# Expert tiles beyond 36 put behind a branch, and none begun in the first unit of a pass

## Chip, core and metric

The kernel runs on one core of a Trainium2 chip. The metric is the device time of one execution in microseconds. The profile is of one execution, taken by the hardware profiler. The engines are TensorE (PE; its weight loads are PEld), VectorE (DVE), ScalarE (ACT), GpSimd (POOL) and SyncE (SP), which issues most of the DMA transfers.

## What is computed

The reference runs two transformer layers over 8 x 256 tokens of width 512, in fp32. Layer 0 adds a linear attention with decays (32 heads of 128, gated, normalized over all heads) and a mixture of experts to its input. Layer 1 adds a small attention and a mixture of 64 low-rank maps.

```
x = x + _L0_attn_ref(xn, ...) + _L0_ffn_ref(xn, ...)
xn = _layernorm(x, axis=-1)
x = x + _L1_attn_ref(xn, ...) + _L1_ffn_ref(xn, ...)
```

The change touches the mixture of experts of layer 0. Each of the 2048 tokens picks 2 of 16 experts:

```
logits = xt @ router_w + router_b
scores = jax.nn.softmax(logits.astype(jnp.float32), axis=-1) + router_bias
g = scores.reshape(T, GROUPS, E // GROUPS)
_, gidx = jax.lax.top_k(g.max(axis=-1), LIM)
...
_, idx = jax.lax.top_k(masked, K)
...
h = jax.nn.silu(xt @ w1 + b1) * (xt @ w2 + b2)
return (y + ge[:, None] * (h @ w3 + b3), None)
```

The reference lets every expert see every token and weights the results with a gate that is zero for all but two experts. The kernel computes only the chosen pairs. How many tokens an expert gets depends on the data.

## The kernel before

**Opening.** The kernel normalizes the tokens, scores them, picks two experts each, and computes the two shared experts. Then it sorts the 4096 (token, expert) pairs into slots, expert after expert, each expert's share rounded up to tiles of 128 slots (lines 495 to 579). Whatever the counts are, no more than NMT = (2048 x 2 + 16 x 127) // 128 = 47 tiles are needed. `ends` (line 546) holds, for each expert, the number of tiles up to and including its own; the last of them is the number of tiles in use. `rows_` and `own_` name the expert whose weights and bias a tile takes; a tile past the last one in use takes expert 15.

**Main loop.** The attention of layer 0 runs in NCH = 4 passes of 512 tokens (i), each with NG = 8 units of four heads (g), and each unit with seven outer products in the order p1, p2, p6, p5, p3, p7, p4 (k = 0 to 6, line 1318). An outer product multiplies one combination of weight blocks with seven combinations of token blocks, on PE at line 735. The weights of two outer products ahead are requested on SP (lines 709 to 712, a ring of three buffers `w`). ACT and DVE empty PSUM, POOL and DVE add the results up. A unit's scores, attention and output projection (lines 857 to 870, 948, 968) are cut into pieces which `later(after, f)` puts on a list; `slot()` (line 755), called once for each small product, takes due pieces from that list, one at a time or two where the list is long. Pieces with names in the tuple at line 762 do not count toward that number.

The instructions of ACT and POOL keep the order in which the code issues them; those of the other engines are ordered by the compiler from the same sequence, by their dependences.

**Expert tiles.** They are such pieces too. `expert(j)` (line 1187) makes an `Expert`, whose two gathers on POOL bring 128 token rows (`xe`) and the weights of the expert (`we`) to a buffer of the pool `stage`, of which there are two; ten slots later `turn` transposes the tokens on PE (line 786), `bias` gathers the bias rows on POOL (792), `up` multiplies (804), with Silu on ACT and one operation on DVE, and `down` multiplies again (816), adds the bias on DVE and stores the result to the rows of tile j of `yd` in DRAM (822). Later, `gather` reads the rows of `yd` that a token's slots name. The same two `stage` buffers also serve the block sums of pass 0, `spare8()` (line 657: at a pass's end, in `load_sum`), and `low_sums`.

The lines 1327 to 1330 hand the tiles out: from the first unit of pass 1 on, at each unit's first outer product, two of them, or three in units 1 to 7 of pass 1; in a first unit (g = 0) they begin 24 slots later than elsewhere. This gives 23 tiles in pass 1, 16 in pass 2 and 8 in units 0 to 3 of pass 3.

**Around a pass's end.** The last unit of a pass queues `combine` (POOL, on the accumulator `acc`), `finish` (DVE, line 646, reads acc) and `store`, which run in the next pass's first unit. There is one `acc`; the next pass first writes it with an ACT copy at line 956.

Of the kernel before, what the change touches and what calls it, by code (L numbers as in the profile page):

```python
# [12 lines left out]
I32 = mybir.dt.int32  # L13
# [7 lines left out]
P = 128  # L21
CH = 512
NCH = NT // CH
# [4 lines left out]
NG = H // HG  # L28
# [4 lines left out]
E, GROUPS, INTER = 16, 4, 128  # L33
# [4 lines left out]

NMT = (NT * TOP + E * (P - 1)) // P
NSLOT = NMT * P  # L40
READ = 32
WROW = 2 * NC * INTER + C + 2
K, TOPK, RANK, SCALING = 64, 16, 16, 2.0
# [27 lines left out]
def block_kernel(  # L71
# [24 lines left out]
    nc = tc.nc  # L96
# [5 lines left out]
    const = ctx.enter_context(tc.tile_pool(name="const", bufs=1))  # L102
# [43 lines left out]
    def once(shape, name, dtype=FP):  # L146
        return work.tile(shape, dtype, tag=name, name=name, bufs=1)
# [31 lines left out]
    dram = ctx.enter_context(tc.tile_pool(name="dram", bufs=1, space=bass.MemoryType.DRAM))  # L179
    yd = dram.tile([NSLOT, C], FP, name="yd")  # L180
    gd = [dram.tile([K, 1, CH], FP, name=f"gd{i}") for i in range(NCH)]
# [10 lines left out]
    xr = [dram.tile([P, TPC, C], FP, name=f"xr{i}") for i in range(NCH)]  # L192
    table = dram.tile([NSLOT, SAME], I32, name="table")
    none = once([P, NMT * SAME], "none", I32)
# [11 lines left out]
    for n in range(WARM):  # L206
# [12 lines left out]
        out=before, in_=before, pattern=[[1, E], [-1, E]], compare_op=ALU.is_gt,  # L219
# [11 lines left out]
        out=dist[:, 0:S], in_=dist[:, 0:S], pattern=[[1, S]], compare_op=ALU.is_ge,  # L231
# [238 lines left out]
    for i in range(NCH):  # L470
        nc.sync.dma_start(
            out=xnd[i * CH : (i + 1) * CH, :].rearrange("(t p) c -> p t c", p=P), in_=xns[i]
# [25 lines left out]
    own_ = const.tile([P, NMT], I32, name="own_")  # L498
    whose = [const.tile([P, n], I32, name=f"whose{n}") for n in (READ, NMT - READ)]

# [3 lines left out]
        out=earlier, in_=earlier, pattern=[[1, P]], compare_op=ALU.is_gt,  # L504
# [35 lines left out]
    ends = disp.tile([P, 1, E], FP, name="ends")  # L540
# [8 lines left out]
    own = disp.tile([P, NMT], FP, name="own")  # L549
    nc.vector.tensor_reduce(own, owner, AX.X, ALU.add)  # L550
    nc.vector.tensor_scalar(own_, own, float(E - 1), None, ALU.min)
    nc.vector.tensor_scalar(own, own, float(E - 1), float(P), ALU.min, ALU.mult)
    nc.vector.tensor_scalar(rows_, own, part, None, ALU.add)

    full = [P, NTT, E]
    slot = disp.tile(full, FP, name="slot")
    nc.vector.tensor_scalar(first, first, float(P), None, ALU.mult)
    tt(slot, pp[:, 0:at].rearrange("p (t e) -> p t e", e=E), first.to_broadcast(full), ALU.add)
    far = disp.tile(full, FP, name="far")
    hit = disp.tile(full, FP, name="hit")  # L560
# [43 lines left out]
    def gather(i, n, y):  # L604

        for t in range(TPC):
# [3 lines left out]
                in_offset=bass.IndirectOffsetOnAxis(ap=slots[:, n, at : at + 1], axis=0),  # L610
                bounds_check=NSLOT - 1, oob_is_err=False,
            )
# [47 lines left out]
    with tc.tile_pool(name="attn", bufs=1) as attn, tc.manual_schedule(engines={mybir.EngineType.Activation, mybir.EngineType.Pool}):  # L660
# [90 lines left out]
        def later(after, f):  # L751
            pieces.append((now[0] + after, len(pieces), f))
            pieces.sort(key=lambda x: x[:2])

        def slot():

            now[0] += 1
            n = 0
            while pieces and pieces[0][0] <= now[0] and n < (2 if len(pieces) > 12 else 1):
                f = pieces.pop(0)[2]  # L760
                f()
                n += getattr(f, "func", f).__name__ not in ("silu", "bias", "gate", "read_table", "take_table", "scatter", "load_sum", "sums1", "sums2", "sums3", "sums4", "settle0", "settle1", "out_sum", "combine", "finish", "store")


        class Expert:


            def __init__(self, j):
# [4 lines left out]
                    out=self.xe, out_offset=None, in_=xnd[:, :],  # L773
                    in_offset=bass.IndirectOffsetOnAxis(ap=whose[j // READ][:, j % READ : j % READ + 1], axis=0),
                    bounds_check=NT - 1, oob_is_err=False,
# [397 lines left out]
                self.result(0, 1, self.a, None)  # L1173

        FROM = NG
        EARLY = 8
        todo = list(range(NMT))
        plan = [(i, g, p) for i in range(NCH) for g in range(NG) for p in ORDER]
        units = []

# [6 lines left out]
        def expert(j):  # L1187
            e = Expert(j)
            later(10, e.turn)
            later(12, e.bias)  # L1190
            later(14, e.up)
            later(19, e.down)

        def scatter(t, n):

            token = small.tile([P, SAME], I32, tag="token", name="token")
            nc.gpsimd.iota(token, pattern=[[0, SAME]], base=t * P, channel_multiplier=1)
            nc.gpsimd.indirect_dma_start(
                out=table[:, :],
                out_offset=bass.IndirectOffsetOnAxis(ap=places[:, n, t : t + 1], axis=0),  # L1200
                in_=token, in_offset=None, bounds_check=NSLOT - 1, oob_is_err=False,
            )

        def read_table(n=0):

            m = min(READ, NMT - n * READ) * SAME
            rows = attn.tile([P, CH], FP, tag="sq", name="rows")[:, 0:m]
            lo = n * READ * SAME
            tc.keep_in_program_order(
# [16 lines left out]
        def low_sums(n):  # L1226

            t0, t1 = (
                staged("low")[:, 0 : 4 * C].rearrange("p (h n) -> p h n", h=2) for _ in range(2)
            )  # L1230
            f = (fa, fb)[n]
            pool = nc.gpsimd

            def store(at, t):
                nc.sync.dma_start(out=low[n][:, at], in_=t)

            def load():
                for at, t in ((3, t0[:, 0]), (2, t0[:, 1]), (0, t1[:, 0])):
                    nc.sync.dma_start(out=t, in_=f[:, at])

            def sums1():
                if n == 0:
                    add(t1[:, 1], t0[:, 0], t0[:, 1], pool)
                else:
                    sub(t1[:, 1], t0[:, 0], t1[:, 0], pool)
                store(1, t1[:, 1])

            def sums2():
                if n == 0:
                    sub(t0[:, 0], t1[:, 0], t0[:, 0], pool)  # L1250
                else:
                    sub(t0[:, 0], t0[:, 1], t0[:, 0], pool)
                store(0, t0[:, 0])

            def sums3():
                if n == 0:
                    sub(t0[:, 1], t1[:, 1], t1[:, 0], pool)
                else:
                    sub(t0[:, 1], t0[:, 1], t1[:, 1], pool)
                store(2, t0[:, 1])  # L1260
                nc.sync.dma_start(out=t1[:, 0], in_=f[:, 1])

            def sums4():
                sub(t1[:, 1], t1[:, 0], t0[:, 1], pool)
                store(3, t1[:, 1])

            load()
            for m, step in enumerate((sums1, sums2, sums3, sums4)):
                later(12 + 9 * m, step)
# [42 lines left out]
        def sevenfold(n):  # L1312

            return plan[n][0] > 0 or plan[n][2] in RAW
# [3 lines left out]
        for n, (i, g, p) in enumerate(plan):  # L1318
            if i == 0 and p == "p5":
                for _ in range(4):  # L1320
                    outers[n + 1].step()
            cur = outers[n]
            u = cur.u
            k = ORDER.index(p)
            if k == 0:
                u.load_decay()
                if i * NG + g >= FROM:
                    for e in range(3 if g > 0 and i * NG + g < FROM + EARLY else 2):
                        if todo:
                            later((24 if g == 0 else 1) + 16 * e, partial(expert, todo.pop(0)))  # L1330
                if i == 0:
                    for e in range(max(5 * g - 3, 0), 5 * g + 2 if g < NG - 1 else 0):
                        later(10 * (e - 5 * g) + 35, partial(scatter, e // TOP, e % TOP))
                    if g == NG - 1:
                        later(4, read_table)
                if i == NCH - 1 and g in (NG - 4, NG - 3):
                    low_sums(g - NG + 4)
                if (i, g) == (NCH - 1, NG - 2):
                    wrapped_up()
            if k == 2:  # L1340
                u.load_decay()
            u.load_out(k)
            last = outers[n - 1] if n and sevenfold(n - 1) else None
            if not sevenfold(n):
                if last:
                    last.p3()
                prepare(n + 2)
                cur.plain(outers[n + 1])
                continue
            if i == 0:  # L1350
                while cur.steps:
                    cur.step()
                cur.following = outers[n + 1]
            cur.p1()
            cur.p7()
            if last:
                last.p3()
            prepare(n + 2)
            cur.p6()
            cur.p4()  # L1360
            cur.p2()
            cur.p5()
# [434 lines left out]
```

## Time and profile before

| | |
|---|---|
| runs shown | 2783.33, 2780.84, 2780.56 us; median 2780.84 us |
| the profiled execution | 2780.53 us, span 2778.5 us (from its first to its last instruction) |
| granted PE clock, mean | 0.997 |
| transposes of expert tiles, L786 | 188 matmuls (4 for each of 47 tiles), 751.8 to 2165.7 us |
| up, L804 | 752 matmuls (16 for each tile) |
| down, L816 | 94 matmuls (2 for each tile) |
| stores to yd, L822 | 47 of 256 KB |
| DMA | 735.87 MB, mean 265 GB/s |

An fp32 product appears as two matmul records, a transpose as one. The records of PE overlap, since matmuls are pipelined: a matmul of 128 columns has a duration of 276 ns but the next one starts 0.11 us later. So what a group of matmuls costs PE is read from start to start, not from the durations. Units are named (pass, unit): (3,0) is the first unit of pass 3. Times in the trace are counted from the start of the span.

### The profile page before, as it was taken

How to read it: one execution, taken by the hardware profiler on the slowest of the kernel's cores; microseconds unless marked ns; L12 is line 12 of the kernel's file. 1: busy time of each engine (PE TensorE's matmuls, PEld its weight loads, DVE VectorE, ACT ScalarE, POOL GpSimd, SP SyncE). 2: the span in 40 equal slices, each digit the busy share in tenths (PEclk: the TensorE clock that was granted, in tenths of full speed). 3: DMA queues.
4: the chain of work that ended last, by engine and by line, in shares of the span. 5: the costliest groups of instructions: out<-in, count | busy, mean ns of one | idle time of the engine just before them, and what ended most of it. 6: DMA issues, size and time to landing. Idle time of an engine off the chain costs nothing.

```text
span 2778.5 us, 49222 instructions
## 1 busy us (share of the span) xinstructions
PE 2733.5 (98%) x19492; PEld 2522.7 (91%) x19492; DVE 1627.6 (59%) x2733; ACT 947.2 (34%) x1683; POOL 1649.8 (59%) x1422
## 2 busy tenths in 40 slices
PE   9999999999999999999999999999999999999999
PEld 5699999999999999999999999999999999987877
DVE  7656777776545555555545555555555555667663
ACT  5232222222433333333343333334433333432221
POOL 6477777776566666665855555556555567553210
PEclk9999999999999999999999999999999999999999
DMA  7898898888977777777877777787877788653211
GB/s 296 310 339 335 311 334 325 337 315 330 352 274 261 288 272 277 265 280 288 304 250 253 253 257 251 264 288 268 281 255 255 270 298 295 218 215 124 78 63 63
DMA packets 155445, 735.87 MB, mean 265 GB/s; under 512 B 18768, under 2 KB 25296, under 8 KB 112848
## 3 DMA queue, kind: packets, MB, share of 16 engines
q1 hardware_dynamic: 137056, 661.89, 64.8%
q0 software_dynamic: 17872, 70.32, 7.7%
q8 instruction: 154, 2.52, 0.4%
q14 instruction: 75, 0.61, 0.1%
q10 hardware_dynamic: 288, 0.52, 0.1%
HBM read 587.84 MB, written 144.04 MB: 263 GB/s over the span
## 4 chain that ended last, share of the span: by engine, by line
PE 86%; DVE 6%; POOL 3%; issue 3%; DMA 2%; ACT 0%; SPq 0%; DVEq 0%; POOLq 0%; ACTq 0%
PE ps_a L735 25%; PE ps_e L735 13%; PE ps_sc L948 10%; PE ps_b L735 7%; PE ps_sc L968 4%; PE ps_o L869 4%; PE ps_sc L857 3%; PE ps_sc L804 3%; PE ps_o L870 2%; PE ps_sc L858 2%; PE ps_a L1676 2%; PE ps_sc L816 1%; DVE w L100 1%; PE ps_a L1579 1%; PE ps_a L359 1%
## 5 line engine op out<-in xcount | busy, mean ns | idle before, releaser
L735 PE MATMUL ps_a<-xt,w 128*128 128x128 f32 x5376 | 751.3, 276 | 16.3 <-DVE r L100 7.6
L735 PEld LDWEIGHTS ps_a<-xt,w 128*128 128x128 f32 x5376 | 686.7, 192 | 46.0 <-issue 14.1
L100 POOL TENSOR_TENSOR c<-c 128x512 f32<-128x512 f32 x240 | 305.2, 1286 | 265.7 <-DVE c L100 263.1
L1103 ACT COPY cp<-ps_a 128x512 f32<-128x512 f32 x384 | 224.0, 584 | 659.9 <-PE ps_a L735 636.9
L100 POOL TENSOR_TENSOR c<-c,r 128x512 f32<-128x512 f32 x264 | 345.8, 1332 | 167.1 <-DVE r L100 166.6
L735 PE MATMUL ps_e<-xt,w 128*128 128x128 f32 x2688 | 374.5, 275 | 0.6 <-DVE r L100 0.3
L735 PEld LDWEIGHTS ps_e<-xt,w 128*128 128x128 f32 x2688 | 341.4, 192 | 6.7 <-issue 2.9
L735 PE MATMUL ps_a<-w,xt 128*128 128x128 f32 x1792 | 346.8, 275 | 0.0
L100 POOL TENSOR_TENSOR w<-w 128x512 f32<-128x512 f32 x224 | 297.7, 1337 | 80.5 <-DVE w L100 32.9
L100 POOL TENSOR_TENSOR sums<-sums,sq 128x512 f32<-128x512 f32 x120 | 155.8, 1298 | 277.4 <-ACT sq L884 276.8
L948 PE MATMUL ps_sc<-wo,gT 128*128 128x256 f32 x1288 | 304.9, 380 | 2.8 <-POOL gT L100 2.8
L735 PEld LDWEIGHTS ps_a<-w,xt 128*128 128x128 f32 x1792 | 272.4, 192 | 0.0
L948 PEld LDWEIGHTS ps_sc<-wo,gT 128*128 128x128 f32 x1288 | 232.9, 190 | 30.9 <-POOL gT L100 3.1
L100 DVE TENSOR_TENSOR acc<-ps_sc,acc 128x512 f32<-128x512 f32 x208 | 142.7, 689 | 195.2 <-PE ps_sc L948 150.6
L891 DVE SCALAR_TENSOR_TENSOR gT<-ps_o,nw,c 128x256 f32<-128x256 f32 x256 | 112.0, 479 | 216.1 <-ACT sq L884 206.0
L735 PE MATMUL ps_b<-xt,w 128*128 128x128 f32 x1536 | 214.8, 276 | 6.5 <-issue 3.7
L100 DVE TENSOR_TENSOR c<-ps_a,c 128x512 f32<-128x512 f32 x216 | 146.8, 687 | 120.7 <-PE ps_a L735 115.4
L735 PEld LDWEIGHTS ps_b<-xt,w 128*128 128x128 f32 x1536 | 195.1, 193 | 9.0 <-issue 5.7
L832 ACT ACTIVATE c<-c 128x512 f32<-128x512 f32 x256 | 150.3, 628 | 146.0 <-DVE c L100 127.9
L884 ACT ACTIVATE sq<-ps_o 128x512 f32<-128x512 f32 x120 | 71.7, 597 | 358.1 <-PE ps_o L870 352.7
L100 DVE TENSOR_TENSOR s<-ps_sc,decay 128x384 f32<-128x384 f32 x256 | 139.7, 553 | 79.9 <-PE ps_sc L858 77.2
L735 PE MATMUL ps_e<-w,xt 128*128 128x128 f32 x896 | 173.5, 275 | 0.0
(297 smaller groups left out, 4723.3 us busy)
## 6 DMA issues: line engine op xcount, KB each, us to landing
w<-in_w_att_dram SPq DMA_DIRECT2D x56, 1024.0 KB
w<-in_w_att_dram SPq DMA_DIRECT2D x72, 768.0 KB
st<-in_w_att_dram SPq DMA_DIRECT2D x32, 1024.0 KB
wo<-in_w_out_dram SPq DMA_DIRECT2D x113, 256.0 KB
decay<-dec SPq DMA_DIRECT2D x64, 384.0 KB
w<-ws0p SPq DMA_DIRECT2D x12, 1792.0 KB
w<-ws1p SPq DMA_DIRECT2D x12, 1792.0 KB
w<-ws2p SPq DMA_DIRECT2D x12, 1792.0 KB
```

What stands on the lines that cost most here:

```text
L100: (eng or nc.vector).tensor_tensor(o, a, b, op)
L735: mm(bank[:, bass.ts(ty, P)], a, b, start=(first and ty == 0), stop=True, skip_group_check=True,)
L804: mm(pu[:, bass.ts(n, P)], w12[:, n, c, :], self.xeT[:, c, :], start=(c == 0), stop=(c == NC - 1),)
L832: nc.scalar.activation(qk, qk, AF.Silu)
L857: mm(p[:, 0:S], self.c[:, 2 * hh, P : 2 * P], q, start=True, stop=True)
L858: mm(p[:, S : S + P], self.c[:, 2 * hh + 1, P : 2 * P], q[:, 1, :], start=True, stop=True,)
L869: mm(po[:, bass.ts(hh, S)], v[:, 0, :], self.s[:, hh, 0:S], start=True, stop=False)
L884: nc.scalar.activation(sq, po, AF.Square)
L891: nc.vector.scalar_tensor_tensor(gT[:, h, :].rearrange("p (t n) -> p t n", t=2), po[:, bass.ts(h, S)].rearrange("p (t n) -> p t n", t=2), ...
L948: mm(py[:, bass.ts(t, S)], self.O[p][:, hh, bass.ts(t, P)], self.wo[p][:, hh, :], start=(t == 0 and hh == 0), stop=(hh == 1), skip_group_c ...
L968: mm(py[:, bass.ts(h, S)], gT[:, hh, bass.ts(t, P)], self.wo[pair, h][:, hh, :], start=(h == 0 and hh == 0), stop=(hh == 1), skip_group_ch ...
L1103: nc.scalar.copy(c, bank)
```

## The change

A constant USUAL = 36 is added. The list of tiles that are handed out to the units ends at 36 instead of 47. The tiles 36 to 46 stand in `beyond()`, called once, at the second outer product of unit (3,3): it loads the number of tiles in use into a register and does the eleven tiles, one after another, inside a branch that is entered only if this number is above 36. The number is kept in a small integer tile, `used`, filled during the routing.

`fill_tile` writes 128 rows of the input x to each of the tiles 36 to 46 of `yd`, one in each of the eleven units from (1,0) on, by a transfer from DRAM to DRAM on SP's queue. Without the branch nothing else writes these rows.

The handing out changes too: a first unit (g = 0) begins no tile, three tiles are begun in units 1 to 4 of pass 1, and two in the other units. This gives 18 tiles in pass 1, 14 in pass 2, and 4 in units 1 and 2 of pass 3.

```diff
+USUAL = 36
...
+    used = const.tile([P, 1], I32, name="used")
+    nc.vector.tensor_copy(used, ends[:, 0, E - 1 : E])
...
-        EARLY = 8
-        todo = list(range(NMT))
+        EARLY = 5
+        todo = list(range(USUAL))
...
+        def fill_tile(j):
+
+            nc.sync.dma_start(out=yd[bass.ts(j, P), :], in_=x[0:P, :])
+
+        def beyond():
+
+            n_used = nc.values_load(used[0:1, 0:1], min_val=0, max_val=NMT)
+            with tc.If(n_used > USUAL):
+                for j in range(USUAL, NMT):
+                    e = Expert(j)
+                    e.turn()
+                    e.bias()
+                    e.up()
+                    e.down()
...
-                    for e in range(3 if g > 0 and i * NG + g < FROM + EARLY else 2):
+                    for e in range(0 if g == 0 else 3 if i * NG + g < FROM + EARLY else 2):
                         if todo:
-                            later((24 if g == 0 else 1) + 16 * e, partial(expert, todo.pop(0)))
+                            later(1 + 16 * e, partial(expert, todo.pop(0)))
+                if FROM <= i * NG + g < FROM + NMT - USUAL:
+                    later(30, partial(fill_tile, USUAL + i * NG + g - FROM))
...
+            if (i, g, k) == (NCH - 1, NG - 5, 1):
+                assert not todo
+                beyond()
             u.load_out(k)
```

The name `fill_tile` is also added to the tuple at line 762.

## The prediction

> **What bounds the kernel now.** I read the engine totals and the clock row, then units side by side, then TensorE's waits.
>
> ```profile
> PE 2733.5 (98%) x19492; PEld 2522.7 (91%) x19492; DVE 1627.6 (59%) x2733; ACT 947.2 (34%) x1683; POOL 1649.8 (59%) x1422
> ...
> PEclk9999999999999999999999999999999999999999
> ```
>
> TensorE (PE) is busy all through, at nearly full clock; nothing else is near. A busy PE can still be waiting, so the proof is in stretches of one unit (seven outer products of one head group), cut at the decay loads of line 1015. Columns: stretch, us, busy us (instructions) of PE, PEld, DVE, ACT, POOL, granted clock, DMA share, GB/s.
>
> ```profile
> 1230.90:1306.70 75.80, 75.80 (x581) 71.97 (x580) 40.86 (x62) 27.53 (x51) 49.44 (x41) 1.00 0.81 299
> ...
> 1674.30:1747.50 73.20, 72.79 (x559) 69.38 (x558) 39.82 (x60) 27.51 (x50) 40.82 (x33) 1.00 0.72 256
> ...
> 2189.50:2256.50 67.00, 66.59 (x515) 64.13 (x514) 36.05 (x54) 26.52 (x48) 43.76 (x31) 1.00 0.75 265
> ```
>
> The first is a unit of pass 1 with three expert tiles, the second one of pass 2 with two, the third one of pass 3 with none. Two tiles cost 73.2 - 67.0 = 6.2 us, 3.1 each, on the path: the unit without tiles is not held up by anything else.
>
> **Eleven tiles leave the path.** Whether they do depends on the routing. The reference's router on its inputs gives experts 2, 5, 6, 8 and 14 the counts 1859, 3, 140, 46 and 2048, and the others none; rounded up to 128 that is 15 + 1 + 2 + 1 + 16 = 35 tiles. 35 is not above 36, so the branch is passed by. The price of a tile, from PE's order of time (start, us, engine, line):
>
> ```profile
> 2165.37 0.60 PE L786 MATMUL ps_sc<-ident,xw 128*128 128x128 f32 x4
> ...
> 2165.81 0.83 PE L735 MATMUL ps_a<-xt,w 128*128 128x128 f32 x6
> ...
> 2169.14 1.95 PE L804 MATMUL ps_sc<-xeT,xw 128*128 128x128 f32 x16
> ...
> 2170.93 0.83 PE L735 MATMUL ps_b<-xt,w 128*128 128x128 f32 x6
> ...
> 2177.12 1.02 PE L816 MATMUL ps_sc<-xw,he 128*128 128x512 f32 x2
> ...
> 2177.98 0.83 PE L735 MATMUL ps_a<-xt,w 128*128 128x128 f32 x6
> ```
>
> Start to next start: turning 0.44, up 1.79, down 0.86, together 3.09 us, which agrees with 3.1 from the units. 11 x 3.09 = 34.0 us off. DVE (0.68 + 0.35 + 0.69 us a tile), ACT (0.37) and POOL (three gathers of 1.0) lose work too, worth nothing while they are beside PE.
>
> A small return: the 2-tile and 0-tile units lose 0.57 us at their last product, the 3-tile units of pass 1 only 0.1 (75.8 - 73.2 is 2.6, not 3.1). Three-tile units fall from seven to four, so +1.5 (0 to 1.5).
>
> **No tile in a pass's first unit.** From 700 to 2200 us PE waited longest thus (us in total, times, longest):
>
> ```profile
> PE ps_a L735 <- DVE r L100: 6.4, 13, 1.3
> PE ps_a L735 <- ACT cp L1103: 3.3, 2, 1.7
> PE ps_sc L948 <- POOL gT L100: 1.6, 1, 1.6
> ```
>
> The two of 1.7 fall at 1364 and 1952, in the first units of passes 2 and 3. Followed back at 1364: the PSUM copies stand behind ACT's L956, which writes acc and waits for the last pass to be read from it:
>
> ```profile
> 1342.95 1.02 POOL L772 DMA_INDIRECT xw<-xnd,whose  x1 [0.16 <-issue]
> 1344.27 1.00 POOL L777 DMA_INDIRECT xw<-in_w_exp_dram,rows__1101  x1 [0.30 <-issue]
> ...
> 1355.37 4.17 POOL L100 TENSOR_TENSOR acc<-acc 128x512 f32<-128x512 f32 x3
> ...
> 1364.81 0.58 ACT L956 COPY acc<-ps_sc 128x512 f32<-128x512 f32 x1 [9.23 <-DVE spare L646]
> ```
>
> POOL combines acc after two gathers of a tile (2.3 us), and DVE copies a tile's xeT (0.68) just before its finish (L646). Without the tile the chain ends 2.3 to 3 us sooner, more than the 1.7: both go, 3.3. The 1.6 (POOL's gT at 1329) comes as POOL falls behind on the bias load in a 3-tile unit; the same border a pass later, after 2-tile units, has no such wait, and unit (1,7) now has two: 1.65 off. The longest of the DVE waits, 1.3 at 773.7 as unit (1,0) ends, comes after a tile's gathers on POOL too (754 to 758); I leave it where it is. Sum -5.0 (0 to -6.3). What is late next there is the same acc chain, 1 us off the path.
>
> **The branch.** No row of before shows one. Queued behind it on PE is the next outer's first product, so all later PE work. Below, 0: the branch could hide in PE's queue. Against that, PE's semaphore rows of 51 ns (L804's, for one) lie between one weight load and the next, not ahead of them, so what PE's sequencer does stands in the line of the work. What is new there: a register read from SBUF, compares, a jump over 11 x 22 = 242 matmuls with as many loads, 484 instructions, and perhaps semaphores to be set right.
>
> ```profile
> q8 instruction: 154, 2.52, 0.4%
> ```
>
> 154 packets of 16 KB carry PE's 38,984 matmuls and loads, 253 each, so the jump spans 1.9 blocks; 0.4% of 16 engines' span over 154 is about 1.15 us a packet. By this row alone a block costs PE nothing: the units show no wait for one. The Trainium skill ("Runtime: NRT & Kernel Launch", Instruction fetch mechanics) speaks against it: fetching ahead is sequential, and a taken branch out of the two loaded blocks stalls until the target is fetched. No run here shows that yet. By the row the branch would be some 0.5 us, by the rule 1.15 us for the packet, about as much again to ask for it (an estimate from the packet), and 1 us for the read and the semaphores: 3 to 4. I take the rule, since the row has only straight code, and 3.5.
>
> Such a pause has a sequel. PE waited 2.03 us at 648.5 and then:
>
> ```profile
> 648.40:652.00 3.60, 1.57 (x12) 1.41 (x12) 2.60 (x4) 0.00 (x0) 1.77 (x3) 0.98 0.89 345
> 652.00:655.40 3.40, 3.40 (x18) 3.40 (x18) 0.91 (x2) 0.00 (x0) 3.40 (x3) 0.51 0.56 170
> 655.40:659.00 3.60, 3.60 (x34) 3.60 (x33) 2.99 (x6) 3.40 (x6) 2.54 (x3) 1.00 0.81 339
> ```
>
> Half the clock for 3.4 us: 18 matmuls where 32 would go, 1.5 us lost. The skill's "TensorE: Matmul & The Clock Gate" (Part 1) asks for an idle window of about 3.4 us before it throttles; by that a pause of 3.5 might cost nothing more, by the row 2.03 was enough (while the 1.7s above were not). The row decides: +1.5. DVE, POOL and ACT jump too, at their own points, with PSUM banks waiting: +1. Branch +6. Upper end: if every engine and transfer must have ended there, a weight load of 1.79 MB at 265 GB/s (6.8 us), POOL's queue (up to 4.65 in one run of adds) and the refill come on top: 20.
>
> **Edits with one answer.** The copy into used is one more DVE operation of 128x1 in the routing before pass 0, like the 0.17 us reciprocal: +0.2. Eleven fill transfers (256 KB, DRAM to DRAM) cost SP 0.33 us of issue each and 0.5 MB read and written in units with room for some 6 MB more (275 GB/s against the 352 of the busiest slice, over 75 us); transfers of 1.5 MB a tile go. SP and the weight ring hide it: PE's waits name no DMA. Without that cover, 2 us each.
>
> **Sum** against the profiled execution, 2780.53 us (span 2778.5 and 2.0 around it; the median of the runs is 2780.84): 2780.5 - 34.0 + 1.5 - 5.0 + 0.2 + 6 = 2749 us.
>
> **Rivals.**
> - The branch is a full meeting of engines and transfers, 20 us: 2763. For it: five engines and in-flight weight loads share that point. Against: nothing behind the branch needs the tiles skipped. 0.10.
> - Work that was hidden anyway: 2772 to 2780. The 67.0 against 73.2 speaks against it. 0.04 (0.03 of it within 0.2%).
> - Slower: after the jump PE's sequential fetching doesn't get ahead again, and every block stalls it. Some 38 blocks follow (685 us, at 154 in 2778). It turns the sign from (2781 - 2749) / 38 = 0.84 us a block; at the 2 us above for a packet and asking for it, it adds 76: 2825. Against: the same fetching costs nothing that shows over the 115 blocks before. 0.06.
> - The branch is taken, so the change doesn't do what it says. Then eleven tiles run with PE empty: gather 5.3 us to landing (the tile's transfers in this unit), then 0.44 + 0.69 + 1.79 + 0.37 + 0.35 + 0.86 + 0.69, some 10 us, or 8 with two buffers overlapped: +88, 2837. It needs more than 36 tiles, and I count 35. 0.02.
>
> **How the numbers follow.** Forecast case 0.78: branch 0 to 12, first units 0 to -6.3, 2740 to 2758. To take in most of the full meeting I end at 2765. A measurement here tells about 0.2% (5.6 us) from no change. Faster: 0.78 + 0.10 + 0.01 = 0.89, less 0.02 for what I haven't seen, 0.87; same 0.03 + 0.01 = 0.04; slower 0.06 + 0.02 + 0.01 = 0.09.
>
> **What will show it.** L786, L804 and L816 with 144, 576 and 72 matmuls; PE 242 fewer. Units of two tiles still 73.2, the first units of passes 2 and 3 near 67 to 68, with L956 no longer waiting 9 us. A hole in PE around 2095 us (2126 less nine tiles and 5), 2 to 5 us long, then 3.4 us near clock 0.5, and no hole at the blocks after it. The prediction is wrong if the hole exceeds 12 us, if PE's waits after it name issue again and again, or if tile instructions show inside it.

## The result, and the profile after

The changed kernel takes 2765.5 us (median of 4 runs, 2763.0 to 2766.5) against 2780.7 before: ratio 0.9938, 95% interval 0.9926 to 0.9949. It is faster, but by 15 us instead of 32, and its median lies half a microsecond above the range, which ended at 2765. The profiled execution took 2766.53 us, span 2764.8. Line numbers are now 3 higher in the main loop (L738 is the old L735, L959 the old L956, L649 the old L646).

The totals and the clock row of the page: PE has lost 242 matmuls, and is as full as before.

```profile
PE 2704.1 (98%) x19250; PEld 2495.3 (90%) x19250; DVE 1618.2 (59%) x2701; ACT 944.2 (34%) x1672; POOL 1618.6 (59%) x1389
...
PEclk9999999999999999999999999999999999999999
```

So the tiles are gone. Where the time is not, stretches of units tell (columns as in the prediction). First before: the first two units of passes 1, 2 and 3, and unit (3,3).

```profile
703.60:772.10 68.50, 68.50 (x532) 65.82 (x531) 35.24 (x56) 29.33 (x50) 40.52 (x34) 1.00 0.90 336
772.10:852.00 79.90, 78.58 (x603) 74.52 (x602) 38.19 (x59) 31.31 (x58) 50.46 (x42) 1.00 0.75 263
1306.70:1376.10 69.40, 66.08 (x500) 62.59 (x499) 36.51 (x57) 25.39 (x45) 50.40 (x42) 1.00 0.84 312
1376.10:1454.80 78.70, 77.80 (x595) 73.67 (x595) 39.47 (x59) 32.58 (x60) 42.65 (x35) 1.00 0.76 266
1893.80:1964.50 70.70, 69.02 (x530) 66.09 (x529) 37.63 (x60) 28.10 (x50) 52.44 (x43) 1.00 0.76 269
1964.50:2043.10 78.60, 77.70 (x594) 73.57 (x593) 39.41 (x58) 32.48 (x60) 42.60 (x35) 1.00 0.76 265
```

The same units after, then (3,3), which was 73.2, and the 3.4 us behind the branch in it:

```profile
705.10:775.00 69.90, 66.44 (x496) 63.27 (x495) 35.72 (x54) 28.24 (x48) 36.35 (x29) 0.98 0.83 317
775.00:851.40 76.40, 76.40 (x590) 73.01 (x591) 36.22 (x55) 31.63 (x59) 49.60 (x41) 1.00 0.78 282
1298.80:1366.00 67.20, 63.51 (x486) 60.64 (x485) 38.67 (x55) 26.95 (x46) 48.95 (x39) 1.00 0.77 283
1366.00:1440.10 74.10, 73.69 (x567) 70.28 (x566) 35.68 (x54) 31.01 (x57) 39.52 (x32) 1.00 0.72 259
1880.20:1952.40 72.20, 68.48 (x514) 65.67 (x513) 40.45 (x58) 29.21 (x51) 49.65 (x39) 0.98 0.69 241
1952.40:2026.50 74.10, 73.69 (x567) 70.28 (x566) 35.87 (x54) 31.22 (x57) 39.56 (x32) 1.00 0.72 259
2099.70:2172.60 72.90, 68.53 (x515) 65.37 (x514) 36.08 (x54) 26.57 (x48) 34.57 (x27) 0.98 0.68 236
2113.90:2117.30 3.40, 3.40 (x8) 2.66 (x9) 0.00 (x0) 0.40 (x1) 0.00 (x0) 0.52 0.62 193
```

The first unit of pass 1 has 36 matmuls fewer and takes 1.4 us more; that of pass 3 has 16 fewer and takes 1.5 us more. In both the clock column has fallen to 0.98: a stretch of 3.4 us at half clock begins at 765.7 and at 1939.9, each right after a wait of PE, and between 700 and 2200 us the kernel before has none. The six units together went from 445.8 to 433.9 us, 11.9 less, though six tiles left them, worth 18.5. The five other tiles behaved: units (1,5) to (1,7) went from 75.8 to 73.5, 73.2 and 73.2, and (3,3) lost two tiles (6.2) and got the branch, 0.3 less in all. Unit (2,5) is 1.0 longer, through one wait. The remainder, 1.5 us more before pass 1 and 3.2 more from unit (3,7) on, is no part of the change that I can name: a second profile of the same changed kernel has 3.3 and 1.4 us less at these two places.

PE's longest waits after (us in total, times, longest):

```profile
PE ps_a L738 <- DVE r L101: 11.6, 20, 1.7
PE ps_a L738 <- ACT cp L1106: 5.8, 3, 2.0
PE ps_o L872 <- DVE s L101: 5.0, 4, 2.6
...
PE ps_sc L951 <- PEq L1204: 4.0, 1, 4.0
```

The two waits behind the ACT copy in first units, 3.3 us, which I had put at nothing, are 4.0 us now (the third of the row lies elsewhere). The last line is the branch. The 2.6 is new; it is in the first unit of pass 1, just before the half clock:

```profile
765.42 0.88 PE L872 MATMUL ps_o<-s,c 128*128 128x256 f32 x2 [2.55 <-DVE s L101]
```

This is the order of time in unit (2,0), on the engines of the wait behind the ACT copy:

```profile
1350.65 2.83 DVE L649 SCALAR_TENSOR_TENSOR spare<-acc,rms,spare 128x512 f32<-128x512 f32 x2
...
1353.59 0.59 ACT L959 COPY acc<-ps_sc 128x512 f32<-128x512 f32 x1 [7.99 <-DVE spare L649]
...
1354.71 0.94 PE L738 MATMUL ps_a<-xt,w 128*128 128x128 f32 x6 [1.98 <-ACT cp L1106]
```

It is the chain of before. Counted from the unit's start (1306.7 and 1298.8), the copy to acc came at 58.1 us before and at 54.8 after: 3.3 sooner, as predicted. But PE began its wait at 57.6 before and at 53.9 after, 3.6 sooner, so the wait grew from 1.7 to 2.0. DVE's steps up to the first finish of the unit show why, before (with PE's wait of then) and after:

```profile
1355.95 0.69 DVE L100 TENSOR_TENSOR c<-ps_e,cp 128x512 f32<-128x512 f32 x1 [0.58 <-PE ps_e L735]
1356.78 0.69 DVE L100 TENSOR_TENSOR c<-ps_b,cp 128x512 f32<-128x512 f32 x1
1357.39 1.02 DVE L646 SCALAR_TENSOR_TENSOR spare<-acc,rms,spare 128x512 f32<-128x512 f32 x1
...
1365.93 0.38 PE L735 MATMUL ps_a<-xt,w 128*128 128x128 f32 x1 [1.67 <-ACT cp L1103]
```

```profile
1345.97 0.69 DVE L101 TENSOR_TENSOR c<-ps_e,cp 128x512 f32<-128x512 f32 x1 [0.59 <-PE ps_e L738]
1346.80 0.69 DVE L101 TENSOR_TENSOR c<-ps_b,cp 128x512 f32<-128x512 f32 x1
1347.40 2.72 DVE L649 SCALAR_TENSOR_TENSOR spare<-acc,rms,spare 128x512 f32<-128x512 f32 x2
```

In both, finish stands behind an add for which DVE waits for PE, so the chain begins with PE: 2.1 us sooner in this unit, where the down of the last tile of the unit before (0.86 us) and PE's wait of 1.65 for gT no longer stand ahead of it. From the first finish on, the chain to the copy is 1.2 us shorter (7.4 and 6.2), as the copy to xeT is gone. But PE's way to the place where it waits is 1.5 us shorter (6.9 and 5.3): the turning and up of the unit's own tile, 2.23 us, are gone, and six other matmuls, 0.67 us, have moved ahead of the place. In unit (3,0) the first finish begins no sooner, and the same two pieces are 1.2 and 1.5 us shorter; there, too, the wait grew from 1.7 to 2.0.

### The profile page after: what moved, and what is told of

The parts are those of the page before. It is cut to its first block, busy times and chain, and to the rows that moved or that the text cites. A ratio compares the mean times of both kernels' runs of the same rounds, so it can differ in the third digit from the quotient of the medians.

```text
span 2764.8 us, 48620 instructions
## 1 busy us (share of the span) xinstructions
PE 2704.1 (98%) x19250; PEld 2495.3 (90%) x19250; DVE 1618.2 (59%) x2701; ACT 944.2 (34%) x1672; POOL 1618.6 (59%) x1389
## 5 line engine op out<-in xcount | busy, mean ns | idle before, releaser
L738 PE MATMUL ps_a<-xt,w 128*128 128x128 f32 x5376 | 752.0, 276 | 21.4 <-DVE r L101 11.6
L738 PEld LDWEIGHTS ps_a<-xt,w 128*128 128x128 f32 x5376 | 686.1, 192 | 52.8 <-DVE r L101 17.2
L738 PE MATMUL ps_e<-xt,w 128*128 128x128 f32 x2688 | 374.7, 275 | 1.2 <-DVE c L101 0.8
L738 PE MATMUL ps_a<-w,xt 128*128 128x128 f32 x1792 | 346.7, 275 | 0.0
L101 POOL TENSOR_TENSOR w<-w 128x512 f32<-128x512 f32 x224 | 297.8, 1337 | 82.8 <-DVE w L101 31.5
L738 PEld LDWEIGHTS ps_e<-xt,w 128*128 128x128 f32 x2688 | 341.5, 192 | 4.9 <-DVE c L101 1.3
L738 PEld LDWEIGHTS ps_a<-w,xt 128*128 128x128 f32 x1792 | 272.4, 192 | 0.0
L738 PE MATMUL ps_b<-xt,w 128*128 128x128 f32 x1536 | 214.7, 276 | 6.2 <-issue 3.7
L738 PEld LDWEIGHTS ps_b<-xt,w 128*128 128x128 f32 x1536 | 196.0, 193 | 9.4 <-issue 5.4
L738 PE MATMUL ps_e<-w,xt 128*128 128x128 f32 x896 | 173.5, 275 | 0.0
```

The lines of the kernel that those rows point to most:

```text
L101: (eng or nc.vector).tensor_tensor(o, a, b, op)
L738: mm(bank[:, bass.ts(ty, P)], a, b, start=(first and ty == 0), stop=True, skip_group_check=True,)
```

## Experiments

The measure is each kernel's ratio to the kernel before, on the same chip; the medians of before there were 2782 to 2784 us. First the changed kernel again, as the base.

> The changed kernel itself once more, beside the next three on the same chip. Both theories: 2763 to 2767 us; runs differ by which waits of about 2 us are followed by a stretch at half clock.

2763.1 us (2762.2 to 2763.5), ratio 0.9925 (0.9913 to 0.9938). The intervals of several kernels below touch this one, so what a piece is worth is read from the units of the traces too.

**No branch.** The call is removed:

```diff
                 assert not todo
-                beyond()
```

> The changed kernel with the branch and its eleven tiles left out altogether (36 tiles, fill transfers kept). Theory A (the branch costs PE its pause of 4.0 us and the half clock after it, 1.7, and nothing else): about 2760 us, 5.7 below the 2765.5 of the changed kernel, unit (3,3) at 67.0 us instead of 72.9. Rival (the branch also spoils the order around it and to the end, and is the reason why only 15 of the 31 us came): about 2750 us.

2755.7 us, ratio 0.9904 (0.9889 to 0.9919). Unit (3,3) is 67.0 us instead of 72.9, so the branch costs 5.9 there. The medians differ by 7 to 10 us, more than that; in this profile the rest is again before pass 1 and behind unit (3,6). The rival's 2750 did not come, and the first units of passes 1 and 3 are still long (72.7 and 71.3 us). The branch, for which I had allowed 6 us, is not where the expected gain went.

**Two tiles in each first unit again**, the other edits kept:

```diff
-        EARLY = 5
+        EARLY = 0
-                    for e in range(0 if g == 0 else 3 if i * NG + g < FROM + EARLY else 2):
+                    for e in range(3 if g > 0 and i * NG + g < FROM + EARLY else 2):
-                            later(1 + 16 * e, partial(expert, todo.pop(0)))
+                            later((24 if g == 0 else 1) + 16 * e, partial(expert, todo.pop(0)))
```

> The changed kernel, branch and all, but with two of the 36 tiles begun in each first unit again, 24 slots late as before, and two in every other unit. Theory C (cover: in a pass's first unit PE waits for the last pass to be finished on POOL and DVE, and the tile begun there was done in time that PE would have waited): the first two units of passes 1 and 3 give back some 3 to 4 us each, 2756 to 2760 us. Rival P (as predicted: a tile's gathers on POOL make that chain late): 2768 to 2771 us, with longer waits in the first units.

2755.2 us (2751.7 to 2760.2), ratio 0.9903 (0.9889 to 0.9916). That is the side of theory C, 6 to 8 us below the changed kernel.

**None in first units, in the kernel before**, with all 47 tiles and no branch:

```diff
-        EARLY = 8
+        EARLY = 16
-                    for e in range(3 if g > 0 and i * NG + g < FROM + EARLY else 2):
+                    for e in range(0 if g == 0 else 3 if i * NG + g < FROM + EARLY else 2):
-                            later((24 if g == 0 else 1) + 16 * e, partial(expert, todo.pop(0)))
+                            later(1 + 16 * e, partial(expert, todo.pop(0)))
```

> The kernel before with all 47 tiles and no branch, but none begun in a first unit (three a unit in units 1 to 7 of passes 1 and 2, five in pass 3). Theory C (cover): the same tiles cost PE their full 3.1 us elsewhere and the first units keep their waits, so slower than before by 6 to 12 us, 2787 to 2793 beside a before of 2781. Rival P (as predicted): 5 us faster, 2776.

2786.9 us against 2783.7, ratio 1.0012 (1.0004 to 1.0020): slower by 3 us, half of what C gave as its least, and not faster as P had it. The three first units are 69.7, 71.3 and 72.1 us, without a tile, against 68.5, 69.5 and 70.7 with one. C had left out that the three-tile units are cheaper by 0.5 us each: they are fourteen here and were seven.

**Combine sooner.** The seven POOL adds at once:

```diff
-                        later(after + n, partial(combine, i, COMBINED[n : n + 1]))
+                        later(after, partial(combine, i, COMBINED[n : n + 1]))
```

> The changed kernel with the seven POOL adds that combine acc queued at once instead of one a slot (passes 1 and 2 end in them). Theory C1 (the acc chain is what PE waits for in first units 2 and 3): the chain ends about 6 us sooner, the waits of 2.0 us behind the ACT copy go, and the half clock after one of them: 2760 to 2762 us. Rival C2 (POOL is short of time there as a whole, so its other adds are late instead): no gain, 2764 to 2768 us, PE waiting for DVE or POOL results instead.

2762.0 us (2761.2 to 2765.9), ratio 0.9928 (0.9915 to 0.9942): no change, though the number lies at the edge of what C1 gave. The last of the adds, which ended at 1934 in unit (3,0) of the changed kernel, ended at 1922.5, and yet ACT waited for the finish nearly as long as before, and PE 1.7 us behind it in both units (2.0 in the changed kernel). From the instructions of L959, the waits in this kernel (us, times; 16.0, 2 in the changed kernel):

```profile
  DVE spare L649: 15.5, 2
```

So POOL's combine, which I had followed the chain back to, was not what came last. What was left is where `finish` stands in the order of DVE's work.

**Finish sooner too**, by four slots:

```diff
-                        later(after + n, partial(combine, i, COMBINED[n : n + 1]))
-                    after += 8
+                        later(after, partial(combine, i, COMBINED[n : n + 1]))
+                    after += 4
```

> The changed kernel with the combine adds queued at once and the four finish operations on DVE queued four slots sooner. In the run with the combine alone the adds ended 12 us sooner and the ACT copy to acc still waited 7.8 us for DVE's finish. Theory C3 (where finish stands in the order of pieces, relative to the first write of acc, sets this wait, and a tile's matmuls between the two covered it): the waits behind the ACT copy in first units 2 and 3 shrink from 2.0 to under 0.5 us: 2758 to 2761 us. Rival (DVE is what is short): DVE results are late instead and the time stays at 2762 to 2766 us.

2754.8 us (2751.6 to 2761.9), ratio 0.9901 (0.9885 to 0.9917), 8 us below the changed kernel beside it. PE's longest wait in the first units of passes 2 and 3 is 0.4 us now: both the waits behind the ACT copy and those of 1.7 for a result of DVE that came 7 to 9 us after them are gone. The same row of L959 now reads:

```profile
  DVE spare L649: 3.1, 1
```

And the first units of passes 2 and 3, 67.2 and 72.2 in the changed kernel:

```profile
1295.50:1359.50 64.00, 63.62 (x490) 61.25 (x490) 36.21 (x55) 27.15 (x46) 47.80 (x39) 1.00 0.83 302
1873.30:1940.70 67.40, 67.02 (x518) 64.56 (x518) 37.48 (x58) 29.39 (x51) 48.41 (x39) 1.00 0.73 257
```

PE is busy nearly all through, and the clock is whole again.

**Both.** Tiles in the first units and the earlier finish:

> Two tiles in each first unit again and combine and finish sooner, both at once, with the branch. Theory C (the tile only covered the wait for acc): once the wait is gone a tile costs its 3.1 us in first units 2 and 3 too, and only the first unit of pass 1, where no acc is waited for, still has cover: 2752 to 2755 us, no sum of the two gains of 8 to 10 us. Rival (the gains are independent): 2745 to 2748 us.

2754.2 us, ratio 0.9900 (0.9884 to 0.9917). The gains of 8 and 8 do not add up; in passes 2 and 3 each repairs the same wait, one by covering it, one by removing it. The six units put side by side (us from decay load to decay load, less 3.09 for each tile handed out in them; six units at 67.0 would make 402) show it best:

| kernel | six units | tiles in them | less the tiles |
|---|---|---|---|
| before | 445.8 | 13 | 405.6 |
| changed | 433.9 | 7 | 412.3 |
| before, none in first units | 439.0 | 8 | 414.3 |
| changed, tiles in first units again | 440.8 | 12 | 403.7 |
| changed, finish sooner | 424.8 | 7 | 403.2 |
| both | 439.7 | 12 | 402.6 |

Five more tiles cost the six units 6.9 us in the changed kernel (440.8 for 433.9), 1.4 each, since part of them falls into time in which PE would have waited. With finish sooner, five cost 14.9 us (439.7 for 424.8), 3.0 each: their full price.

**Tiles in the first unit of pass 1 alone**, with the earlier finish:

```diff
-                    for e in range(0 if g == 0 else 3 if i * NG + g < FROM + EARLY else 2):
+                    for e in range((2 if i == 1 else 0) if g == 0 else 3 if i * NG + g < FROM + EARLY else 2):
```

> Combine and finish sooner, and two tiles begun in the first unit of pass 1 alone. Theory C: the 2.6 us that PE waits there for DVE's scores are covered, first units 2 and 3 stay at 64 and 67 us: 2751 to 2753 us. Rival (a tile's gathers on POOL make those scores late): 2756 to 2758 us.

2751.4 us, ratio 0.9890 (0.9873 to 0.9906). No `combine` runs in that unit, and the copy to acc does not wait there for `finish`, but PE waited 2.6 us there for DVE's scores (L872 in the waits above) and ran at half clock after it; with the tiles this is covered, and the unit is 68.4 us instead of 69.8. The next unit is longer, 79.9 for 76.4, so the two tiles cost 2.1 us in both units together and not 6.2.

**The branch elsewhere.** It was moved into unit (3,0), whose waits it was to cover: to the last outer product, k = 6, and then to k = 5.

```diff
-            if (i, g, k) == (NCH - 1, NG - 5, 1):
-                assert not todo
+            if (i, g, k) == (NCH - 1, 0, 6):
```

> The changed kernel with the branch moved from unit (3,3) to the last outer product of the first unit (3,0), just ahead of where PE waits 2.0 us for the ACT copy to acc. Theory C: POOL and DVE catch up while PE stands at the branch, so the 2.0 us there, the 1.7 at the next product and their half clock (1.6) fall into the branch's pause: 2761 to 2763 us. Rival (a pause costs its 4.0 + 1.7 wherever it stands, since all engines stop): 2765 us, and the wait for the ACT copy stays.

2762.7 us, ratio 0.9930 (0.9917 to 0.9944), the same as in its old place. The number lies in theory C's range, the mechanism does not hold: both waits of 2.0 us stand in the trace, just before the branch.

> The changed kernel with the branch at the last but one outer product of unit (3,0), ahead of the waits for acc and not after them as in the run before (2762.7 us, where the waits of 2.0 and 2.0 us stood before the branch). Theory C: POOL and DVE go on with combine and finish while PE stands, so both waits shrink to under 0.5 us: 2757 to 2760 us. Rival (a pause adds wherever it stands): 2762 to 2764 us, the waits keep their 2.0 us.

2767.4 us, ratio 0.9951 (0.9936 to 0.9966), slower than the changed kernel and than either theory. Unit (3,0) is 82.8 us. The waits around it:

```profile
DVE spare L649 <- POOL acc L101: 8.3, 1, 8.3
...
PE ps_a L738 <- ACT cp L1106: 7.2, 1, 7.2
...
PE ps_sc L951 <- DVE gT L894: 4.2, 1, 4.2
```

DVE now has the first finish ahead of gT, stands 8.3 us for POOL's combine, and so PE waits for gT. Everything that the code issues ahead of the branch must come before it on each engine, which pulls finish forward past work that is more urgent. That this is the cause is read from the trace; no run isolates it. The 7.2 is the wait behind the branch itself, which took PE 5.1 us here.

**A shorter branch.** Four tiles in it instead of eleven:

```diff
-                for j in range(USUAL, NMT):
+                for j in range(USUAL, USUAL + 4):
```

> The changed kernel with only four tiles in the branch instead of eleven (tiles 40 to 46 are left out; no slots lie in them here). PE's jump is then 176 instructions, less than one 16 KB packet of code. Theory F (the pause is the fetch of the target, which lies beyond the loaded code): the compare-and-branch on PE falls from 5.2 us to well under 1.5, the pause from 4.0 to under 1 and the half clock goes: unit (3,3) about 67.5 us instead of 72.9, 2758 us. Rival (every taken jump fetches anew, or the pause is the register read and the semaphores): pause and time as in the changed kernel, 2763 to 2765 us.

2756.6 us (2756.0 to 2756.8), ratio 0.9908 (0.9891 to 0.9924). What the engines did at the branch, first in the changed kernel (median ns in the middle):

```profile
L1204 SPq COMPARE_BRANCH  x1: 53/53/53, 2104.5 to 2104.5; - x1
L1204 POOLq COMPARE_BRANCH  x1: 45/45/45, 2105.4 to 2105.4; - x1
...
L1204 PEldq COMPARE_BRANCH  x1: 5207/5207/5207, 2108.4 to 2108.4; - x1
L1204 ACTq COMPARE_BRANCH  x1: 45/45/45, 2109.0 to 2109.0; - x1
...
L1204 DVEq COMPARE_BRANCH  x1: 72/72/72, 2109.7 to 2109.7; - x1
```

and PE with four tiles:

```profile
L1204 PEldq COMPARE_BRANCH  x1: 236/236/236, 2106.7 to 2106.7; - x1
```

The register reads differ little (0.46 to 0.54 us on the five engines), so PE's 5.2 us is the jump over 484 instructions, and a jump over 176 costs 0.24. During the long one the trace has two packets of 16 KB on PE's instruction queue, at 2109.5 and 2110.2, lasting 1.0 and 1.9 us. In all nine profiles with the long branch a packet of PE's code begins 0.9 to 2.7 us after the branch, and PE goes on 1.3 to 1.5 us after the last has landed; during this short one none begins. That speaks for theory F; no run changed the place of the target alone. SP, too, waited at the long branch,

```profile
SPq L1204 <- SPq L1204: 8.3, 1, 8.3
```

and with four tiles it goes on within 0.5 us. Unit (3,3) is 67.4 us with four tiles, 0.4 above a unit without branch, and no half clock follows.

**Three short branches.** The last kernel has the earlier finish, the tiles in the first unit of pass 1, and all eleven tiles in three branches:

```diff
-        def beyond():
+        def beyond(first):
-            with tc.If(n_used > USUAL):
-                for j in range(USUAL, NMT):
+            with tc.If(n_used > first):
+                for j in range(first, min(first + 4, NMT)):
...
-            if (i, g, k) == (NCH - 1, NG - 5, 1):
+            if (i, g) == (NCH - 1, NG - 5) and k in (1, 3, 5):
                 assert not todo
-                beyond()
+                beyond(USUAL + 2 * (k - 1))
```

> The run before (combine and finish sooner, tiles in the first unit of pass 1) with the eleven tiles in three branches of four, four and three, at the second, fourth and sixth outer product of unit (3,3), so that each jump on PE is shorter than a packet of code; all 47 tiles are still computed where they hold slots. Theory F: each branch costs PE 0.2 to 0.5 us and no half clock, unit (3,3) is 67.5 to 68.5 us instead of 74.0, 2745 to 2747 us. Rival (three meetings of SP with all its transfers, 8 us each, or a fetch at one of the three after all): 2750 us or more.

2745.8 us (2741.3 to 2747.0), ratio 0.9865 (0.9848 to 0.9881). It computes all that the kernel before computes and is the fastest of all here. SP goes on within 0.5 us at each of the three branches, and no packet of PE's code begins during one. The three branches, and unit (3,3):

```profile
L1204 PEldq COMPARE_BRANCH  x3: 221/236/447, 2095.3 to 2140.6; - x3
```

```profile
2087.20:2155.40 68.20, 67.28 (x514) 64.34 (x513) 36.05 (x55) 26.62 (x48) 34.59 (x27) 1.00 0.67 240
```

## Why the prediction was right and where it failed

- **Which bound.** Right: PE is 98% busy in both kernels, and outside first units a removed tile gave its 3.1 us.
- **35 tiles, branch passed.** Right: 19250 matmuls, 242 fewer, none of a tile inside the branch.
- **34.0 us for eleven tiles, +1.5 back.** Right for the five that left units (1,5) to (1,7) and (3,3): 7.5 us in the first three, where 3 x 3.09 less 1.5 makes 7.8. Wrong for the six of the first two units of each pass, which gave 11.9 and not 18.5.
- **First units, -5.0.** This is the step that failed: "Without the tile the chain ends 2.3 to 3 us sooner, more than the 1.7: both go". The chain did end sooner, by 3.3 us in pass 2 and 1.2 in pass 3, but neither wait went; both grew from 1.7 to 2.0. I had moved the chain and left PE where it was. The tile stood in PE's way as well: without it the chain is 1.2 us shorter from the first finish on, and PE's way to the same place 1.5. Nor was POOL's combine what came last, but the place of finish on DVE: adds 12 us sooner changed nothing; with finish four slots sooner as well, 9 us went out of the four units of passes 2 and 3. What I called late next, the acc chain "1 us off the path", was still on it. The same thought was missing for pass 1, where no acc is waited for: there two tiles had covered a wait for DVE's scores. In the first two units of passes 1, 2 and 3 I expected 6.2, 9.5 and 7.8 us off (tiles and waits), and 2.1, 6.8 and 3.0 came. The difference, 11.6 us of the 17 that were missing in the profile, is 4.1 for pass 1 and 7.5 for passes 2 and 3, with a stretch of half clock in each of passes 1 and 3.
- **The wait of 1.65 at gT.** It went; only the 1.1 of a later place is left in that row.
- **The branch, +6.** Right in its sum, 5.9 in unit (3,3): a pause of 4.0 for my 3.5, then 3.4 us at clock 0.52. That sequel does not decide between the row of before (2.03 us was enough) and the Trainium skill's "TensorE: Matmul & The Clock Gate" (Part 1), which puts the throttle after an idle window of about 3.4 us: the pause was longer than both. The wait of 1.98 us in unit (3,0) does decide, for the row: half clock followed. The parts of the pause were off. I took 1.15 us for a packet and as much for asking; PE's branch took 5.2. That only 4.0 of it shows is due to work still queued: PE's sequencer read the register at 2107.8 and its array worked until 2109.9, so the sequencer does run ahead, which I had ruled out. That a jump out of the loaded code stalls, the rule of the Trainium skill's "Runtime: NRT & Kernel Launch" (Instruction fetch mechanics), agrees with the 5.2 us, the 0.24 us and the packets; the row of straight code would have been the wrong guide. The 1 us for other engines is not seen.
- **Copy, fill transfers.** Nothing seen of them: no wait of PE names a DMA in either profile.
- **Rivals.** Of the full meeting only a part came, for SP alone: its 8.3 us at the branch end when the weight load that it issued just ahead has landed (the last packet at 2112.84), and the weight ring hides this from PE. Fetching got ahead again at once; units (3,4) and (3,5) take the same 67.0 us as before.

About 6 us of the missing 17 are left outside first units: 1.0 in unit (2,5), and 4.7 before pass 1 and behind unit (3,6), which differ as much between two profiles of the same kernel. Why DVE's scores come 2.6 us late in unit (1,0) was covered, not explained.

## What to carry to other kernels

Before you count removed work as gained, ask in each place where it stood whether the engine waits there or soon after. If so, that work was cover, and removing it moves the engine to the wait sooner; remove the wait, by moving what releases it up in the order, and then the work is worth its price. When you advance a chain, advance in the same sum the engine that waits for it. A branch to pass by rare work was cheap here where its jump was shorter than a packet of code: cut a long one into short ones.

## What the hardware showed that was not expected

A compare-and-branch took 45 to 72 ns on four engines and 5.2 us on PE, for a jump over 484 instructions; over 176 it took 0.24 us. In the other kernels with the long branch it took from 3.4 to 5.1.

A wait of 2 us is sometimes followed by 3.4 us at half clock, which loses about 1.5 us, and sometimes not. In the profile of the changed kernel, the same wait of 1.98 us in unit (2,0) was followed by matmuls at full pace, and in unit (3,0) by the half clock. The traces show what differs. In each of the 14 profiles the half-clock stretches begin on one grid of 3.413 us: between their starts lie whole multiples of it, to within 3 ns. Taken by windows of that grid, from 100 to 2700 us and at full clock, all 50 windows in which PE's rows show 1.95 us or more without a matmul were followed by half clock, and none of the 10509 with less than 1.75; between these, 9 of 13 were. The wait in (3,0) lies in one window with its whole 1.98 us, that in (2,0) with 1.87. In the kernel before, the waits behind the ACT copy were 1.7 us, and the clock stayed whole behind them. That runs of one kernel differ by several us is not explained by this: the two profiles of the changed kernel differ by 4.3 us in span and have their stretches from pass 1 on at the same four places.
